# A sparse graph layer on one core: another order of sixteen units in the second stage, one early load of rows, an early drain of GpSimd and a last store by ScalarE

## The chip, the cores and the metric

The kernel runs on one core of a Trainium2 chip. Its time is the device time of one launch in microseconds; the median of three runs is 1491.0 us (1484.07 to 1491.29). The profile shown here is one more execution, which took 1490.79 us; its trace spans 1488.3 us from the first to the last instruction.

## What is computed

The reference, cut to what matters (x is 8 x 4096 x 256, adj is 4096 x 4096 with few entries that are not zero, W is 256 x 256, all float32):

```python
HW = einsum('bnf,fo->bno', x, W)
A_norm = relu((adj + adj.T) * 0.5)
D = sum(A_norm, axis=1)
DAD = D**-0.5 [:, None] * A_norm * D**-0.5 [None, :]
out = relu(einsum('nm,bmo->bno', eye(N) - DAD, HW))
result = layernorm(x + out, axis=-1)
```

Nodes with low numbers have many neighbours, nodes with high numbers few. The kernel uses that: for each block of output rows it gathers only the rows of HW that have an entry there.

## The kernel before, in words

**First stage** (to about 565 us). It reads adj, makes it symmetric, writes it to a buffer in HBM (`a_dram`), sums the degrees, forms g = r * (x W) for every block of 128 nodes and writes it to `g_dram` (8 KB for one node: 8 batches of 256). It also finishes the product of output block 0 (`lead`) and prepares the lists of the first units of `SEQ`.

**Second stage** (from about 565 us). The other 31 blocks of 128 output rows are taken in 16 *units*. Unit u has blocks 2u+1 and 2u+2, called b0 and b1 below; unit 15 has one block. They are taken in the order of the list `SEQ`; before the change that is 1 to 9, then 0, then 10 to 15. Low numbers are heavy, with 0 the heaviest.

- A unit needs `tiles` gathered tiles. A tile is 128 rows of g (`gather`, L959, 1 MB) and the matching pieces of adj (L951), both by indirect DMAs that GpSimd issues. Rows that a list doesn't fill aren't fetched. The tiles lie in a ring of `RING` = 12 buffers: `gather_ahead` asks for the next tile as soon as the oldest one has been used for the last time. Two "hub" blocks of g stay in SBUF.
- TensorE works a unit off in *steps*, in an order that `steps_of` fixes. A step is one full product of a tile (128x128, four banks), or a round in which up to eight small products of 64x32 run beside each other on parts of the array, with one to five tiles (`tiled`). Both are one pass over four PSUM banks. Blocks b0 and b1 have four banks each.
- When a block is complete, ScalarE evicts its four banks to y (`evict`, L767; there is one y buffer). VectorE adds the rows of x (L777), makes the statistics, the inverse root and the normalised rows (L786 to L810); SyncE stores them (`store`, L820). Rows of x come through `residual` (L761), issued by ScalarE into a pool of four buffers, the first block's after three steps of a unit and the second's after five (`after(6, ...)`, `after(10, ...)`; each step counts two).
- The lists of later units are made on the way. In the unit at place n of SEQ, VectorE runs `prepare` (patterns of the unit at n+4, and `spread` of that at n+2), and then, one step after b0 is complete, TensorE runs the counting products of `lists` (L293, L294, L376, L377, L430). They borrow two banks of b0. VectorE reads them (`index`, `place_rest`, `place`), and only then can the next unit's b0 begin. In the last places there is less of this: no patterns from place 12 on, and no lists at all from place 14 on.
- Every engine works in order, and `queue(...)` puts instructions behind the last one traced on an engine. ScalarE also carries a nop for each pass of a tiled step (`ticks`, L1201), which TensorE waits for two passes later.

**The end.** `finish_last` treats the last block in four parts: eviction by ScalarE, additions by GpSimd and VectorE, the inverse root by GpSimd (L1039), the normalisation by ScalarE (L1048), and one store for each part by SyncE (L1055). A flag is then read, which decides on a fallback that isn't taken with this input, and all engines drain and meet (L1323).

Of the kernel before, what the change touches and what calls it, by code (L numbers as in the profile page):

```python
# [20 lines left out]

KINDS = [15, 1, 4, 2, 8, 16, 64, 32, 128, 240, 51, 204, 60, 195, 0]

SEQ = [*range(1, 10), 0, *range(10, 16)]

HUBS = [2] * 16

# [40 lines left out]
def kernel(  # L68
# [25 lines left out]
    nc = tc.nc  # L94
    B, N, F = x.shape
    FO = w.shape[1]
    P = 128
# [6 lines left out]
    NU = NB // 2  # L104
# [4 lines left out]
    HOLD = 10  # L109
    RING = 12  # L110
    REACH = 5
    EPS = 1e-5
    NK = len(KINDS)
    L = 64
# [355 lines left out]
    with (  # L470
# [181 lines left out]

        due = [[n + 1, constants, (u,)] for n, u in enumerate(SEQ)]

# [43 lines left out]
        for i in range(NS):  # L698
            diag = stat1.tile([P, A, P], F32, tag="diag", name=f"diag_{i}")
            for j in range(i, NS):  # L700
                tij = load_adj(i, j)
                tji = load_adj(j, i) if j > i else tij
                parts = [(i, j, tij, tji)] + ([(j, i, tji, tij)] if j > i else [])
                parts = [(p, spool.tile([P, A, S], F32, tag="sym", name=f"sym_{p[0]}_{p[1]}")) for p in parts]
# [29 lines left out]
            if i in (1, 2, 3, 4):  # L734
                u = SEQ[i - 1]
# [6 lines left out]
            if i in (2, 4):  # L742
                u = SEQ[i // 2 - 1]
                at = 4 if i == 2 else 0
# [14 lines left out]
    def residual(i, engine):  # L759
        xr = blocks_pool.tile([P, B, F], F32, tag="adj", name=f"xr_{i}")  # L760
        engine.dma_start(xr, x[:, i * P : (i + 1) * P, :].rearrange("b p f -> p b f"))  # L761
        return xr
# [56 lines left out]
    def store(i, z):  # L819
        nc.sync.dma_start(out[:, i * P : (i + 1) * P, :].rearrange("b p f -> p b f"), z)  # L820
# [72 lines left out]
    with (  # L893
# [18 lines left out]
        steps = [(u, step) for u in SEQ for step in steps_of(u)]  # L912
# [14 lines left out]
        def queue(engine):  # L927

            traced = reversed(nc.cur_bb.bb.instructions)
            return tc.issue_after(next(i for i in traced if i.engine == engines[engine]))  # L930
# [38 lines left out]
        def gather_ahead():  # L969
            nonlocal asked, eaten  # L970
            while eaten < asked and not uses_left[order[eaten]]:
                eaten += 1
            while asked < len(order) and asked - eaten < RING:
                gather(asked)
                asked += 1
            if asked == len(order) and asked - eaten < RING and NB - 1 not in xr:
                xr[NB - 1] = ring[asked % RING].rearrange("p (b f) -> p b f", b=B)
                with queue("pool"):
                    nc.gpsimd.dma_start(
                        xr[NB - 1], x[:, (NB - 1) * P :, :].rearrange("b p f -> p b f")  # L980
                    )


        later = []

        def after(n, fn, *args):
            later.append((n, fn, args))
# [7 lines left out]

        u = SEQ[0]
        xr = {i: residual(i, nc.sync) for i in (0, *range(2 * u + 1, 2 * u + 1 + blocks(u)))}
# [10 lines left out]
        def finish_last(i):  # L1008

            z, banks = xr.pop(i), py.pop(i)  # L1010
            y = ypool.tile([P, B, FO], F32, tag="y", name=f"y_{i}", bufs=1)
            n = S // FO
            parts = [slice(c * n, (c + 1) * n) for c in range(G // S)]
            for c, bs in enumerate(parts):
                with queue("act"):
                    nc.scalar.activation(
                        y[:, bs].rearrange("p b o -> p (b o)"),
                        banks[c],
                        AF.Relu,
                        scale=minus_r[:, i : i + 1],  # L1020
                    )

            with queue("pool"):
                nc.gpsimd.tensor_add(z[:, parts[0]], z[:, parts[0]], y[:, parts[0]])
            with queue("dve"):
                nc.vector.tensor_add(z[:, parts[1]], z[:, parts[1]], y[:, parts[1]])
            stats = []
            for c in range(len(parts) + 1):
                if c < len(parts):
                    if c == 2:  # L1030
                        with queue("dve"):
                            nc.vector.tensor_add(z[:, parts[3]], z[:, parts[3]], y[:, parts[3]])
                    with queue("dve"):
                        mv, rstd = statistics(i, z[:, parts[c]], stat, f"_{c}")
                    if c == 0:
                        with queue("pool"):
                            nc.gpsimd.tensor_add(z[:, parts[2]], z[:, parts[2]], y[:, parts[2]])
                    with queue("pool"):
                        nc.gpsimd.tensor_tensor(rstd, rstd, neg_half[:, :n], ALU.pow)  # L1039
                    stats.append((mv, rstd))  # L1040
                if c == 0:
                    continue
                bs, (mv, rstd) = parts[c - 1], stats[c - 1]
                shift = stat.tile([P, n], F32, tag="shift", name=f"shift_{c - 1}")
                with queue("dve"):
                    nc.vector.scalar_tensor_tensor(shift, mv[:, :, 0], -1.0, rstd, ALU.mult, ALU.mult)
                for b in range(n):
                    nc.scalar.activation(  # L1048
                        y[:, bs.start + b, :],
                        z[:, bs.start + b, :],  # L1050
                        AF.Identity,
                        bias=shift[:, b : b + 1],
                        scale=rstd[:, b : b + 1],
                    )
                nc.sync.dma_start(out[bs, i * P : (i + 1) * P, :].rearrange("b p f -> p b f"), y[:, bs])  # L1055

        def finish(i):

# [22 lines left out]
        def exchange(rows):  # L1081

            if finished:
                with queue("sp"):
                    store(*finished.pop(0))
            for i in rows:
                with queue("act"):
                    xr[i] = residual(i, nc.scalar)


        ahead = {u: {k: SEQ[n + k] for k in (2, 3, 4) if n + k < NU} for n, u in enumerate(SEQ)}

        def prepare(u):
            if 2 in ahead[u]:
# [109 lines left out]
        for q, (u, step) in enumerate(steps):  # L1204
            new = q == 0 or steps[q - 1][0] != u
            if new:
                after(6, prepare, u)
                rows = [2 * u + 1 + b for b in range(2)] if q > 0 and blocks(u) == 2 else []
                if q == 0:
                    after(8, exchange, [])  # L1210
                elif rows:
                    after(6, exchange, rows[:1])
                    after(10, exchange, rows[1:])
                else:
                    after(2, exchange, [])
                    after(4, exchange, [])
                left, begun = {}, set()
                for v, st in steps[q:]:
                    if v == u:
                        for _, _, b, j in st:  # L1220
                            for e in range(QU) if j is None else [j]:
                                left[b, e] = left.get((b, e), 0) + 1
                for b in range(blocks(u)):
                    py[2 * u + 1 + b] = []
            touched = sorted({b for _, _, b, _ in step})
            for b in touched:
                if not py[2 * u + 1 + b]:
                    py[2 * u + 1 + b] = [
                        psum.tile([P, S], F32, tag=f"b{b}", name=f"py_{u}_{b}_{c}") for c in range(NC)
                    ]  # L1230
            if step[0][1] is None:
                (op,) = step
                b = op[2]
                hs = {(b, e) for e in range(QU)}
                assert not hs & begun or hs <= begun
                for h in hs:
                    left[h] -= 1
                for c in range(NC):
                    product(
                        u, op, c, slice(0, P), slice(0, P), not hs & begun, not any(left[h] for h in hs)  # L1240
                    )
                begun |= hs
            else:
                for op in step:
                    assert op[2:] in begun
                    left[op[2:]] -= 1
                last = [op for op in step if not left[op[2:]]]
                tiled(u, step, last)
            for op in step:
                t = op[0]  # L1250
                uses_left[u, t] -= 1
                if t < 0:
                    load_hub_rows(SEQ[SEQ.index(u) + 1 :], -1 - t, op[2])
            gather_ahead()
            run_later(2)
            for b in touched:
                if not any(left[b, e] for e in range(QU)):
                    if b == 0:
                        after(2, lists, u)
                    finish(2 * u + 1 + b)  # L1260
# [11 lines left out]
    with tc.If(short > 0):  # L1272
        with (
# [4 lines left out]
            for i in range(NB):  # L1278
# [16 lines left out]
                y = evict(i, py, ypool)  # L1295
# [32 lines left out]
```

## Time and profile before

| | |
|---|---|
| median of three runs | 1491.0 us |
| the profiled execution | 1490.79 us |
| its span | 1488.3 us |
| mean granted TensorE clock | 0.974 |
| moved by DMA | 541.85 MB, 364 GB/s over the span |

The second stage by units, in the order of SEQ. Tiles and steps follow from the tables `CAPS` and `FIRST` through `steps_of`. Start and length run from the first matmul of the unit to that of the next one. Idle is TensorE's idle time in it, V is VectorE's busy time, DMA the share of the 16 DMA engines.

| unit | tiles | steps | start us | length us | idle us | V us | DMA |
|---|---|---|---|---|---|---|---|
| 1 | 22 | 21 | 582.5 | 83.8 | 4.1 | 22.9 | 1.01 |
| 2 | 19 | 18 | 666.3 | 64.9 | 0 | 44.8 | 0.96 |
| 3 | 19 | 17 | 731.2 | 61.1 | 0 | 42.2 | 1.00 |
| 4 | 18 | 15 | 792.3 | 56.0 | 1.9 | 48.5 | 0.98 |
| 5 | 17 | 15 | 848.3 | 53.9 | 0 | 45.2 | 1.02 |
| 6 | 17 | 14 | 902.2 | 55.8 | 2.8 | 45.2 | 1.00 |
| 7 | 16 | 13 | 958.0 | 52.3 | 2.7 | 45.3 | 1.02 |
| 8 | 17 | 12 | 1010.3 | 51.3 | 3.4 | 45.9 | 1.00 |
| 9 | 16 | 12 | 1061.6 | 51.3 | 4.1 | 45.0 | 0.98 |
| 0 | 27 | 28 | 1112.9 | 107.2 | 3.3 | 44.9 | 0.92 |
| 10 | 14 | 12 | 1220.1 | 45.0 | 1.6 | 41.6 | 0.90 |
| 11 | 15 | 12 | 1265.1 | 49.5 | 5.8 | 45.6 | 1.00 |
| 12 | 15 | 11 | 1314.6 | 51.6 | 7.4 | 47.9 | 0.99 |
| 13 | 13 | 11 | 1366.2 | 39.5 | 0 | 26.7 | 1.02 |
| 14 | 13 | 11 | 1405.7 | 38.5 | 0 | 22.4 | 1.00 |
| 15 | 7 | 5 | 1444.2 | 24.2 | 2.8 | 14.6 | 0.63 |

How to read the profile: a page gives each engine's busy time, in tenths in 40 equal slices of the span too. "PEclk" is the clock that TensorE was granted. A row of the waits says which engine waited, at which line, for whom, how long in total, how often, and how long at most. A row of the timeline gives start, duration, engine, line and operation of instructions put together, and in brackets the idle time before them and what ended it. Ends of matmuls are modelled, so that a wait of TensorE can lie inside its busy time; the starts tell more.

### The profile page before, as it was taken

Reading aid. Unit: us, or ns where it says so; the run is one execution under the profiler, and the core shown is the slowest. Engines: PE = TensorE matmul, PEld = TensorE weight load, DVE = VectorE, ACT = ScalarE, POOL = GpSimd, SP = SyncE. Lnnn points to the kernel's source line nnn. Section 1 sums busy time; section 2 is a strip of 40 time slices with the busy share of each in tenths; the row PEclk is TensorE's granted clock in tenths of the full one; section 3 lists DMA queues with packets and bytes.
Section 4 is the critical chain, followed back from the end, with each engine's and each line's share of the span. In section 5 each row is a group of like instructions: output and inputs, shape, how many; then the busy total and the mean of one; then the engine's idle time right before and its main releaser. Section 6 shows DMA issues by size and latency. Waiting matters only on the chain.

```text
span 1488.3 us, 29574 instructions
## 1 busy us (share of the span) xinstructions
PE 1381.5 (93%) x10960; PEld 749.5 (50%) x10960; DVE 1042.9 (70%) x3174; ACT 360.8 (24%) x462; POOL 761.4 (51%) x1556
## 2 busy tenths in 40 slices
PE   7998988979998998999999999999989999988993
PEld 6777877756777763343433333333333334433341
DVE  4668569879687763219486897788889029999654
ACT  4555554444544460000101101100100010011111
POOL 2445010010322336765775777777767557777761
PEclk9999999999999999999999999999999999998996
DMA  9999999998999999999999999999999889999994
GB/s 348 364 377 380 403 365 358 387 388 314 357 361 354 368 388 379 390 400 337 370 379 358 375 401 374 382 394 378 348 387 386 312 292 383 370 352 398 393 369 144
DMA packets 216694, 541.85 MB, mean 364 GB/s; under 512 B 19070, under 2 KB 108862, under 8 KB 182110
## 3 DMA queue, kind: packets, MB, share of 16 engines
q0 software_dynamic: 55200, 282.68, 49.1%
q1 hardware_dynamic: 93472, 126.89, 24.7%
q10 hardware_dynamic: 67872, 130.32, 23.1%
q8 instruction: 89, 1.46, 0.4%
q14 instruction: 61, 0.50, 0.1%
HBM read 434.91 MB, written 136.34 MB: 384 GB/s over the span
## 4 chain that ended last, share of the span: by engine, by line
PE 53%; DMA 23%; DVE 16%; issue 5%; ACT 2%; POOL 1%; ACTq 0%; DVEq 0%; POOLq 0%
PE py L1166 33%; PE pg L606 9%; DMA g<-g_dram,gi 7%; DMA a_dram<-sym 6%; DVE sym L499 3%; PE lead L564 3%; PE tr L495 3%; PE xtr L595 3%; DMA xin<-in_x_dram 3%; DMA out_dram<-xr 2%; DMA xr<-in_x_dram 2%; DMA ga<-a_dram,ai 2%; DVE stats L786 2%; DVE xr L810 1%; DVE xr L777 1%
## 5 line engine op out<-in xcount | busy, mean ns | idle before, releaser
L1166 PE MATMUL py<-g,ga 64*32 64x512 f32 (+1 forms) x7072 | 612.4, 610 | 23.1 <-DMA g<-g_dram,gi 22.0
L1166 PEld LDWEIGHTS py<-g,ga 64*32 64x32 f32 (+1 forms) x7072 | 226.8, 114 | 392.1 <-issue 314.7
L959 POOL DMA_INDIRECT g<-g_dram,gi x265 | 297.7, 1124 | 113.6 <-issue 71.0
L951 POOL DMA_INDIRECT ga<-a_dram,ai x265 | 282.9, 1068 | 136.2 <-PE py L1166 64.1
L767 ACT ACTIVATE y<-py,minus_r 128x512 f32<-128x512 f32 x120 | 72.7, 688 | 789.1 <-PE py L1166 634.4
L606 PE MATMUL pg<-w_sb,xt 128*128 128x256 f32 x1024 | 229.7, 383 | 4.2 <-ACT xt L596 4.2
L1166 PE MATMUL py<-g_hub,gh 128*128 128x512 f32 x496 | 229.2, 604 | 3.8 <-DVE pos_k L239 3.8
L606 PEld LDWEIGHTS pg<-w_sb,xt 128*128 128x128 f32 x1024 | 194.8, 193 | 30.5 <-ACT xt L596 5.0
L499 DVE TENSOR_TENSOR sym<-tr,adj 128x512 f32<-128x512 f32 x256 | 162.8, 683 | 57.4 <-PE tr L495 40.6
L506 DVE TENSOR_REDUCE sums<-sym 128x64 f32<-128x2048 f32 x64 | 145.3, 2279 | 62.4 <-ACT sym L503 62.4
L1166 PEld LDWEIGHTS py<-g_hub,gh 128*128 128x128 f32 x496 | 91.2, 191 | 136.3 <-issue 123.5
L495 PE MATMUL tr<-ident,adj 128*128 128x128 f32 x1024 | 135.9, 280 | 21.4 <-DVE sym L499 14.8
L503 ACT ACTIVATE sym<-sym 128x2048 f32<-128x2048 f32 x64 | 122.6, 1915 | 113.6 <-DVE sym L499 101.2
L507 POOL TENSOR_SCALAR uses<-sums 128x64 uint8<-128x64 f32 x64 | 24.8, 388 | 239.5 <-DVE sums L506 203.5
L442 DVE TENSOR_SCALAR low<-lists 128x17 f32<-128x17 f32 (+8 forms) x14 | 2.5, 175 | 200.0 <-PE lists L430 200.0
L495 PEld LDWEIGHTS tr<-ident,adj 128*128 128x128 f32 x1024 | 115.2, 143 | 53.7 <-DVE sym L499 32.5
L777 DVE TENSOR_TENSOR xr<-xr,y 128x2048 f32<-128x2048 f32 x31 | 70.9, 2286 | 54.7 <-ACT y L767 42.0
L595 PE MATMUL xtr<-ident,xin 128*128 128x128 f32 x512 | 72.8, 291 | 21.3 <-DVE sym L499 12.3
L810 DVE TENSOR_SCALAR xr<-xr,mv,root 128x256 f32<-128x256 f32 x248 | 87.6, 425 | 1.1
L786 DVE BATCH_NORM_STATS2 stats<-xr 128x6 f32<-128x256 f32 x248 | 84.1, 412 | 1.1
L564 PE MATMUL lead<-gt,strip 128*128 128x512 f32 x176 | 83.2, 593 | 0.0
L596 ACT COPY xt<-xtr 128x512 f32<-128x512 f32 x128 | 68.0, 592 | 60.0 <-PE xtr L595 58.6
(157 smaller groups left out, 1057.7 us busy)
## 6 DMA issues: line engine op xcount, KB each, us to landing
adj<-in_adj_dram SPq DMA_DIRECT2D x64, 1024.0 KB, 10.2
a_dram<-sym ACTq DMA_DIRECT2D x64, 1024.0 KB, 8.9
out_dram<-xr SPq DMA_DIRECT2D x31, 1024.0 KB, 23.6
xr<-in_x_dram ACTq DMA_DIRECT2D x28, 1024.0 KB, 15.1
xin<-in_x_dram SPq DMA_DIRECT2D x44, 512.0 KB, 11.9
g_dram<-gt ACTq DMA_DIRECT2D x22, 1024.0 KB, 8.9
xin<-in_x_dram POOLq DMA_DIRECT2D x20, 512.0 KB
g_dram<-held ACTq DMA_DIRECT2D x10, 1024.0 KB, 14.1
```

The source lines that it names most:

```text
L495: ins = nc.tensor.transpose(pt[:, c * P : (c + 1) * P], tji[:, c, a * P : (a + 1) * P], ident)
L499: nc.vector.tensor_add(sym[:, a, :], pt, tij[:, a, :])
L503: nc.scalar.activation(sym, sym, AF.Relu, scale=0.5)
L506: nc.vector.tensor_reduce(sums, sym.rearrange("p a (c q) -> p a c q", q=E), AX.X, ALU.add)
L564: nc.tensor.matmul(lead[c], lhsT=strip, rhs=g[:, c * S : (c + 1) * S], start=not done, stop=len(done) == NB - 1, skip_group_check=True,)
L595: nc.tensor.transpose(pt[:, k, c, :], xin[b // H][:, b % H + k, c * P : (c + 1) * P], ident)
L606: ins = nc.tensor.matmul(pg[:, k * FO : (k + 1) * FO], lhsT=xt[:, b + k, c, :], rhs=w_sb[:, c, :], start=(c == 0), stop=(c == FC - 1),)
L786: nc.vector.bn_stats(stats[:, b, :], z[:, b, :])
L810: nc.vector.tensor_scalar(z[:, b, :], z[:, b, :], mv[:, b, 0:1], rstd[:, b : b + 1], ALU.subtract, ALU.mult,)
L951: nc.gpsimd.indirect_dma_start(out=at if both else at[:, : E if one else P], out_offset=None, in_=a_pairs if both else a_groups if one els ...
L959: nc.gpsimd.indirect_dma_start(out=gt, out_offset=None, in_=g_dram, in_offset=bass.IndirectOffsetOnAxis(ap=gi[:, t : t + 1], axis=0), boun ...
L1166: return nc.tensor.matmul(py[2 * u + 1 + b][c][cols, :], lhsT=at[ps, off + cols.start : off + cols.stop], rhs=gt[ps, c * S : (c + 1) * S], ...
```

## The change

Four edits.

1. `SEQ` takes the units in another order: 2, 4, 3, 5, 11, 7, 6, 1, 12, 0, 13, 10, 14, 9, 8, 15. The first stage follows, since it prepares the lists of the first four of them.
2. In a unit of at least `LONG` = 28 steps (only unit 0 has so many) both blocks of x of the unit behind it are loaded after 14 steps (`load_rows`, ScalarE's queue). `exchange` in that next unit still stores, and finds the rows there.
3. GpSimd gets a `drain` behind its last gathers and the load of the last block's rows.
4. The fourth and last store of `finish_last` is issued by ScalarE in place of SyncE.

```diff
-SEQ = [*range(1, 10), 0, *range(10, 16)]
+SEQ = [2, 4, 3, 5, 11, 7, 6, 1, 12, 0, 13, 10, 14, 9, 8, 15]
...
+    LONG = 28
...
                     nc.gpsimd.dma_start(
                         xr[NB - 1], x[:, (NB - 1) * P :, :].rearrange("b p f -> p b f")
                     )
+                with queue("pool"):
+                    nc.gpsimd.drain()
...
-                nc.sync.dma_start(out[bs, i * P : (i + 1) * P, :].rearrange("b p f -> p b f"), y[:, bs])
+                engine = nc.sync if c < len(parts) else nc.scalar
+                engine.dma_start(out[bs, i * P : (i + 1) * P, :].rearrange("b p f -> p b f"), y[:, bs])
...
+            load_rows(rows)
+
+        def load_rows(rows):
+
             for i in rows:
-                with queue("act"):
-                    xr[i] = residual(i, nc.scalar)
+                if i not in xr:
+                    with queue("act"):
+                        xr[i] = residual(i, nc.scalar)
...
-        ahead = {u: {k: SEQ[n + k] for k in (2, 3, 4) if n + k < NU} for n, u in enumerate(SEQ)}
+        ahead = {u: {k: SEQ[n + k] for k in (1, 2, 3, 4) if n + k < NU} for n, u in enumerate(SEQ)}
...
+                if sum(v == u for v, _ in steps) >= LONG:
+                    v = ahead[u][1]
+                    after(LONG, load_rows, [2 * v + 1 + b for b in range(2)])
```

## The prediction

> **What bounds the kernel now.** I read the page's slices first, then the second stage cut at the units' first matmuls, then the waits, then TensorE's timeline around each wait, and the last lines at the end. Slices (40 of 37.2 us):
>
> ```profile
> PE   7998988979998998999999999999989999988993
> DVE  4668569879687763219486897788889029999654
> PEclk9999999999999999999999999999999999998996
> DMA  9999999998999999999999999999999889999994
> ```
>
> The first stage barely depends on the edits, so I look at slices 15 to 39. DMA is at its top all the way but for slices 31 and 32 (the first is 0), where VectorE shows 0 and 2: that is unit 0 (1112.9 to 1220.1 us). Right behind it VectorE is at 9.
>
> The second stage by units (length, then busy us of each engine, clock, DMA share); the rows are units 8, 9, 0, 10, 11, 12, 13, 14:
>
> ```profile
> 1010.30:1061.60 51.30, 47.95 (x566) 17.75 (x564) 45.94 (x170) 4.84 (x8) 39.71 (x38) 0.97 1.00 379
> 1061.60:1112.90 51.30, 47.18 (x449) 18.38 (x445) 44.99 (x171) 4.84 (x8) 36.88 (x37) 0.97 0.98 361
> 1112.90:1220.10 107.20, 103.92 (x861) 39.42 (x860) 44.87 (x169) 4.84 (x8) 66.06 (x65) 0.98 0.92 345
> 1220.10:1265.10 45.00, 43.40 (x510) 19.00 (x508) 41.64 (x157) 4.84 (x8) 30.19 (x29) 1.00 0.90 344
> 1265.10:1314.60 49.50, 43.68 (x466) 19.66 (x462) 45.58 (x170) 4.84 (x8) 36.88 (x35) 0.99 1.00 373
> 1314.60:1366.20 51.60, 44.22 (x455) 17.59 (x451) 47.88 (x172) 4.84 (x8) 38.69 (x36) 0.87 0.99 375
> 1366.20:1405.70 39.50, 39.50 (x408) 15.79 (x401) 26.71 (x95) 4.93 (x9) 28.98 (x27) 1.00 1.02 392
> 1405.70:1444.20 38.50, 38.50 (x370) 14.93 (x369) 22.44 (x82) 6.35 (x11) 24.57 (x24) 1.00 1.00 369
> ```
>
> VectorE's work is about 45 us a unit, heavy or light, until the lists run out (units 13, 14). Who waits:
>
> ```profile
> DVE low L442 <- PE lists L430: 200.0, 14, 60.0
> PE py L1166 <- DMA g<-g_dram,gi: 22.0, 11, 3.5
> ```
>
> VectorE waits for TensorE 200 us in total, 60 of it in unit 0; elsewhere TensorE waits for it. TensorE's timeline:
>
> ```profile
> 993.42 8.65 PE L1166 MATMUL py<-g,ga 64*32 64x512 f32 x124 [2.69 <-DMA g<-g_dram,gi]
> ...
> 1047.77 5.34 PE L1166 MATMUL py<-g,ga 64*32 64x512 f32 x60 [2.66 <-DMA g<-g_dram,gi]
> ...
> 1264.26 0.95 PE L430 MATMUL lists<-val,hot 128*128 128x30 bf16 x32
> ...
> 1305.48 3.70 PE L1166 MATMUL py<-g_hub,gh 128*128 128x512 f32 x8
> 1313.29 0.36 PE L293 MATMUL lists<-kind,ones 128*128 128x448 bf16 x1 [4.11 <-DVE kind L283]
> ...
> 1313.73 0.99 PE L430 MATMUL lists<-val,hot 128*128 128x26 bf16 x32
> ```
>
> So three limits lie close together. **P**: unit 3 (17 steps, no wait) took 61.1 us; less about 1.25 for its lists that is 3.52 us a step, so P = 3.52 x steps + 1.25. **V**: behind unit 0 the lists of units 10, 11, 12 (L430 at 1215.8, 1264.3, 1313.7, 1359.2) follow at 48.4, 49.5 and 45.4 us, VectorE solid between them: no unit with full list work is shorter than about 48.5. **D**: from 582.5 to 1468.4 us the gathers' queue takes 76.6% of the DMA engines' time, 678 us for 265 tiles or 2.56 a tile; stores and row loads take 10.1 and 10.0%, 178 us for 31 blocks, 11.5 a unit.
>
> Last, the end's line L1323:
>
> ```profile
> L1323 POOLq DRAIN  x3: 46/103/8321, 1479.2 to 1488.1; - x3
> L1323 SPq DRAIN  x3: 7/7/7, 1485.3 to 1487.8; - x3
> ```
>
> GpSimd's drain runs from 1479.2 to 1487.5; SyncE, which waits for the last store, is through at 1485.4.
>
> **What the Trainium skill says.** "Perfetto Trace Analysis", Optimization Strategy: where the most-contended engine changes over time, interleaving the regimes may help. The trace agrees that there are such regimes (unit 0 against 10 to 12). "TensorE: Matmul & The Clock Gate", Part 1: after an idle window of about 3.4 us the array runs at half clock until it has been busy as long. It agrees: the step around the 2.69 us wait above took 8.4 us (989.7 to 998.1) at clock 0.80, against 3.5; a wait costs nearly twice its length. "DMA: Bandwidth & Descriptors", Queues, rings and completion order: the engines go round the queues. It agrees: from 1130 to 1140 us loads, gathers and stores had 38.4, 36.6 and 31.3%, where gathers had 96.9% from 1160 to 1180; a wait in unit 0 follows at 1148. No page prices GpSimd's drain.
>
> **The change, part by part.** Each sum is against the profiled 1490.8 us, which is practically the median.
>
> (a) *Places 0 to 9, up to the tenth lists.* Before: 582.5 to 1215.8, 633.3 us, with units 1 to 9 and 0, 165 steps. Ten units, nine lists' 1.25 and a last step behind the lists: 164 x 3.52 + 11.3 = 588.6, losses 44.7. They are: 8.8 at the start (first round, five tiles: 12.3 us for 3.5), 2.2 in unit 4 (VectorE, behind unit 3), 4.9, 4.8, 8.6, 7.1 and 7.0 in units 6, 7, 8, 9, 0 (gathers), and about 1.3 in small ones. After: units 11 and 12 for 8 and 9, one step less, 163 x 3.52 + 11.3 = 585.1. Losses: start 6.2 (unit 2's first round needs four tiles, and a tile's two issues take 2.57 us on GpSimd); 2.2 behind unit 3; 11 has P = 43.5 against V = 48.5, so 5.0; 12 has 40.0, so 8.5; 7 keeps its 4.8, since its tiles 125 and 126 could not be asked for before 979.2 and are used at 989.7; unit 6 2 (D = 17 x 2.56 + 11.5 = 55 against P = 50.5, with unit 11 and 7 ahead of it); unit 0 4, since its queue is fuller. Sum 32.7, so 617.8: **-15.5**. Bounds: losses of 24 to 45, so -24 to -3.
>
> (b) *Places 10 to 12.* Units 13, 10, 14 for 10, 11, 12: one step less, but VectorE's work belongs to the place and not to the unit. P is 40.0, 43.5, 40.0, all under V. 143.3 us remain: **0** (-3 to +3).
>
> (c) *Places 13 to 15.* Before: 1359.2 to 1468.4, 109.2 us. Units 9 and 8 in place of 13 and 14: two steps more, **+7.0**. D is 52.5 and 55.0 against P of 43.5: the queue falls 20 us behind, against 5.3 + 6.3 in units 13 and 14, which had no wait. The ring is 12 x 2.56 = 31 us deep and full after (b), but some of it isn't usable, since unit 9's tile 159 gets its buffer at 1082.9 and is needed at 1091.7. Units 9 and 8 lost 7.1 and 8.6 before; from a full queue I take 3 for each. **+13** in all (+7 to +22). Unit 15's own 6 us wait I leave.
>
> (d) *Rows of unit 13 in the middle of unit 0.* Two loads of 1 MB, 88.6 / 28 = 3.2 us of the DMA engines each, go where the share falls to 0.60 (1174 to 1188), and leave unit 13's start. Unit 13 waits for VectorE, so **0**. They stand in ScalarE's queue ahead of L1201's nops: if their buffers weren't stored by then, TensorE would stand. About 50 us into unit 0 the stores of the unit before are gone (gathers alone from 1160), which hides it; without that cover some 5 us.
>
> (e) *Drain.* It goes where GpSimd is idle from 1448.2 to 1469.3, 21 us for 8.3; behind it in its queue is only L1024. The second and third drain took 0.10 and 0.05 us, so I take the last one as short. SyncE then ends it: **-2.1** (0 if it costs 8.3 again).
>
> (f) *Last store by ScalarE.* SyncE issued it at 1480.55, 0.03 behind the last activation; it saves a semaphore and the queue behind the third store: **-0.1** (0 to -0.6).
>
> Sum: 1490.8 - 15.5 + 0 + 13 - 2.2 = **1486**.
>
> **Rivals.** *Forecast* (0.40): as above; own range 1479 to 1494. *The queue stays full* (0.30): (a) loses only 26 and reaches -22, and a full ring carries 9 and 8, (c) +8: 1490.8 - 22 + 8 - 2.2 = 1475. For it: DMA falls short only in units 2, 0, 10 and 15. Against: the waits of units 7 and 9 come from buffers, not from bandwidth. *Tail starves* (0.20), the slower side: 9 and 8 stand where no heavy unit follows; of the 20 us only some 10 are covered (unit 14 was 11.6 behind, and unit 15 waited), the rest costs nearly double through the clock. Then (c) is 7 + 16 = +23, and (a) about -11 for the same reason: 1490.8 - 11 + 23 - 2.2 = 1501. It decides once (c) exceeds (a)'s gain by 10. *The order does nothing* (0.10): VectorE's floor in places 4, 8 and 10 to 12 eats what unit 0 gave; only the end gains: 1489.
>
> **How the numbers follow.** A measurement here can tell about 0.5% (7.5 us) from no change: 1483.5 and 1498.5 are the borders. Faster: nearly all of the second case and a third of the first, 0.42. Slower: most of the third, 0.18. Same: 0.40. The range reaches from below the second case to the third: 1469 to 1502.
>
> **What would show it.** Lists at 48 to 50 us in places 4, 8, 10, 11; the tenth lists some 13 to 18 us earlier; TensorE waiting for gathers in units 9 and 8 near the end; GpSimd's last drain under 1 us. I am wrong if light units behind heavy ones run at 40 to 44 us between lists, or if 9 and 8 run at 43 us or above 55.

## The result, and the profile after

The changed kernel takes 1492.25 us (median of 17 runs, 1486.62 to 1498.57) against 1488.79 us for the kernel before (17 runs, 1484.07 to 1496.77): a ratio of 1.0038 [1.0025, 1.0051]. It is slower by some 0.4% (the two medians differ by 0.2%, 3.5 us), where 0.3% faster was forecast. The time lies inside the stated range, but on the other side of the kernel before. (Some experiments below ran where the kernel before itself took 1739 to 1743 us at a mean clock near 0.92 in place of 0.97, so each ratio holds only beside its own time of the kernel before, and most experiments stand twice, the second time beside 1484 to 1490 us.)

The profiled execution took 1492.11 us, with a span of 1490.0 us and a mean clock of 0.972. Cut as the prediction cuts it, in us of the two profiled executions (a *place* is a position in `SEQ`, counted from 0; places 0 to 9 are called the front below, places 13 to 15 the tail):

| stretch | before | after | difference | forecast |
|---|---|---|---|---|
| start of the second stage | 582.5 | 583.7 | +1.2 | 0 |
| (a) to the tenth lists | 633.4 | 624.0 | -9.4 | -15.5 |
| (b) to the thirteenth lists (places 10 to 12) | 143.3 | 142.9 | -0.4 | 0 |
| (c) to the last matmul | 109.2 | 124.2 | +15.0 | +13 |
| (e), (f) from there to the end | 20.0 | 15.2 | -4.8 | -2.2 |
| span | 1488.3 | 1490.0 | +1.7 | -4.7 |

The start of the second stage lies anywhere from 580 to 588 us in the profiles of these kernels, whose first stages hardly differ, so its 1.2 us mean nothing. The two spans differ by 1.7 us where the medians differ by 3.5: the sums below hold to a few us, and it is the two large entries, -9.4 and +15.0, that have to be explained.

The slices of the kernel after:

```profile
PE   7998998979999999999999999999979997998985
DVE  4667568789597752257958979965699058999417
PEclk9999999989999999999999999999989998998998
DMA  9999999999999999999999999999999978999995
```

The dip of DMA hasn't gone. From slices 31 and 32 it has moved to 32 and 33 (1192 to 1266 us), the end of unit 0 and the light unit 13. VectorE shows 0 in slice 31, inside unit 0, then 5, 8 and 9: in unit 13 the others wait for it, as the next two views show. The units 6, 12, 0, 13, 10, 14, 9, 8 and 15 of the kernel after (length, then busy us of PE, PEld, DVE, ACT and POOL, clock, DMA share, GB/s):

```profile
926.30:983.70 57.40, 54.06 (x486) 20.25 (x485) 45.07 (x169) 4.85 (x8) 42.08 (x41) 0.97 1.01 384
1059.70:1110.10 50.40, 41.27 (x454) 17.09 (x452) 46.02 (x173) 4.85 (x8) 35.91 (x34) 0.90 0.98 361
1110.10:1212.10 102.00, 101.47 (x869) 38.41 (x862) 44.07 (x169) 4.85 (x8) 61.01 (x60) 1.00 0.97 361
1212.10:1262.60 50.50, 42.05 (x405) 16.64 (x404) 46.17 (x171) 4.85 (x8) 33.59 (x30) 0.90 0.82 293
1262.60:1306.30 43.70, 43.34 (x510) 19.12 (x508) 40.38 (x156) 4.84 (x8) 30.47 (x27) 1.00 0.89 343
1306.30:1357.50 51.20, 42.59 (x408) 16.75 (x405) 47.40 (x172) 6.42 (x11) 37.02 (x36) 0.90 1.00 382
1357.50:1403.60 46.10, 43.83 (x441) 18.57 (x440) 26.81 (x96) 3.38 (x7) 28.57 (x27) 1.00 0.94 319
1403.60:1457.20 53.60, 48.92 (x529) 18.35 (x527) 22.83 (x83) 4.79 (x8) 39.90 (x39) 0.94 0.99 381
1457.20:1474.80 17.60, 17.60 (x128) 6.81 (x120) 16.33 (x69) 2.42 (x4) 0.00 (x0) 1.00 0.56 204
```

Units 13 and 14 took 39.5 and 38.5 us at the end of the old order, with 27 and 22 us of VectorE's work. In places 10 and 12 they take 50.5 and 51.2, with 46 and 47 of it. TensorE's timeline shows why (in order of time: a line of unit 6, one of unit 12, two of unit 13, two of unit 8):

```profile
963.85 11.62 PE L1175 MATMUL py<-g,ga 64*32 64x512 f32 x140 [2.76 <-DMA g<-g_dram,gi]
...
1104.01 0.56 PE L294 MATMUL lists<-kind,ones 128*128 128x448 bf16 x1 [9.13 <-DVE kind L284]
...
1243.58 3.70 PE L1175 MATMUL py<-g_hub,gh 128*128 128x512 f32 x8
1255.73 0.56 PE L294 MATMUL lists<-kind,ones 128*128 128x448 bf16 x1 [8.45 <-DVE kind L284]
...
1427.80 13.05 PE L1175 MATMUL py<-g,ga 64*32 64x512 f32 x170 [1.70 <-DMA g<-g_dram,gi]
...
1444.74 5.35 PE L1175 MATMUL py<-g,ga 64*32 64x512 f32 x60 [2.23 <-DMA g<-g_dram,gi]
```

In unit 13 TensorE stands 8.45 us until VectorE has the patterns for the lists (L284), and in unit 12 it stands 9.13 us. In units 6 and 8 it waits for gathers: 2.76, then 1.70 and 2.23 us. At the end, the drains of the kernel after (duration in ns, minimum, median and maximum, then first and last start):

```profile
L984 POOLq DRAIN  x1: 17057/17057/17057, 1453.9 to 1453.9; - x1
...
L1335 POOLq DRAIN  x3: 34/47/103, 1483.7 to 1489.7; - x3
L1335 SPq DRAIN  x3: 7/7/7, 1489.1 to 1489.5; - x3
```

The early drain (L984) takes 17.06 us, twice the 8.32 of the old one. It ends at 1471.0, and GpSimd's next work is at 1475.8, so it costs nothing. The first of the three at L1335, which took the 8.32 us before, takes 0.05 us.

**One balance for all orders.** Every order has the same 227 steps, so only losses differ. A unit's loss is what it took over 3.52 us a step and over the 1.25 us or so of the lists made in it. From the three profiles (the third is f3_tail_back, an experiment below):

| units | before | after | f3_tail_back |
|---|---|---|---|
| first unit (1; 2; 2) | 8.7 | 2.8 | 1.0 |
| the others of 1 to 5 | 2.0 | 3.4 | 2.7 |
| 6 and 7 | 10.5 | 12.9 | 11.5 |
| 8 and 9 | 15.6 | 14.3 | 16.9 |
| 0 | 7.4 | 2.2 | 2.6 |
| 10, 11, 12 | 19.1 | 17.4 | 19.0 |
| 13 and 14 | -0.4 | 21.8 | -0.4 |
| 15 | 6.6 | 0.0 | 3.6 |
| sum | 69.5 | 74.8 | 56.9 |

The change pays 22.2 us in units 13 and 14, and elsewhere it saves 16.9 on balance, chiefly in the first unit, in unit 0 and in unit 15.

### The profile page after: what moved, and what is told of

Read it like the earlier page. It is cut to its first block, busy times and chain, and to the rows that moved or that the text cites. A ratio compares the mean times of both kernels' runs of the same rounds, so it can differ in the third digit from the quotient of the medians.

```text
span 1490.0 us, 29565 instructions
## 1 busy us (share of the span) xinstructions
PE 1378.9 (93%) x10960; PEld 751.3 (50%) x10960; DVE 1041.4 (70%) x3174; ACT 360.7 (24%) x462; POOL 773.9 (52%) x1556
## 4 chain that ended last, share of the span: by engine, by line
PE 48%; DVE 23%; DMA 20%; issue 4%; ACT 2%; POOL 2%; ACTq 0%; DVEq 0%; POOLq 0%
PE py L1175 29%; DMA g<-g_dram,gi 9%; PE pg L607 8%; DMA a_dram<-sym 6%; PE lead L565 5%; DVE sym L500 3%; DMA xin<-in_x_dram 3%; PE tr L496 3%; PE xtr L596 3%; DVE stats L787 2%; DVE xr L778 2%; DVE xr L811 2%; DVE sums L507 2%; DVE hot L410 1%; DMA ga<-a_dram,ai 1%
## 5 line engine op out<-in xcount | busy, mean ns | idle before, releaser
L952 POOL DMA_INDIRECT ga<-a_dram,ai x265 | 295.4, 1115 | 139.5 <-PE py L1175 66.0
L960 POOL DMA_INDIRECT g<-g_dram,gi x265 | 295.2, 1114 | 111.7 <-issue 64.7
L811 DVE TENSOR_SCALAR xr<-xr,mv,root 128x256 f32<-128x256 f32 x248 | 84.2, 411 | 1.1
## 6 DMA issues: line engine op xcount, KB each, us to landing
a_dram<-sym ACTq DMA_DIRECT2D x64, 1024.0 KB, 10.9
```

Of the source, the lines that this page charges most:

```text
L811: nc.vector.tensor_scalar(z[:, b, :], z[:, b, :], mv[:, b, 0:1], rstd[:, b : b + 1], ALU.subtract, ALU.mult,)
L952: nc.gpsimd.indirect_dma_start(out=at if both else at[:, : E if one else P], out_offset=None, in_=a_pairs if both else a_groups if one els ...
L960: nc.gpsimd.indirect_dma_start(out=gt, out_offset=None, in_=g_dram, in_offset=bass.IndirectOffsetOnAxis(ap=gi[:, t : t + 1], axis=0), boun ...
```

## The experiments

The theory to be tested: the loss sits in the order of the places behind unit 0. VectorE's list work stays with the place, so light units put there are stretched, and units 9 and 8, which lose time to their gathers, do so at the end as well. The rivals: the transfers as a whole (stores and gathers) bind; or the edits at the end or the early rows cost what the order gave.

### The edits one by one

e1_end_only and f6_end_only, the same edit, the order and the rows as before:

```diff
-SEQ = [2, 4, 3, 5, 11, 7, 6, 1, 12, 0, 13, 10, 14, 9, 8, 15]
+SEQ = [*range(1, 10), 0, *range(10, 16)]
-    LONG = 28
+    LONG = 99
```

> The order of before, with GpSimd's early drain and the last store by ScalarE; no early load of rows. Theory (the change is a sum: front -9, middle 0, tail +15, end -3 to -5): from the last activation to the end 5.0 us in place of 7.8, so about -2.8 us, ratio 0.998. Rival (the end was shorter because VectorE had finished the last block but one earlier, not through the drain): that stretch stays near 7.8 us and the time within 1 us.

> The order of before, the early drain and the last store by ScalarE, no early load. Theory: the stretch behind the last matmul falls by the 2.9 us that separate kernels with and without these edits elsewhere (15.2 against 18.0), to about 17; ratio 0.998. Rival (the gain is VectorE's being done earlier in the new order): stretch 20 us, ratio 1.000.

Measured: e1 0.9988 [0.9967, 1.0009] (1739.88 us beside 1742.58 for the kernel before) and f6 0.9968 [0.9938, 0.9999] (1734.71 beside 1738.64). From the last matmul to the end both profiles have 15.1 us, against 18.0 in e2_order_only, f4_order_only and others that lack the two edits: -2.9 us. For f6 about 17 had been expected. The kernel before has 20.0 because VectorE is late there (see f3_tail_back), which it isn't in these two runs. The end alone wasn't timed beside 1490 us.

e2_order_only and f4_order_only, the new order alone in the kernel before:

```diff
-SEQ = [*range(1, 10), 0, *range(10, 16)]
+SEQ = [2, 4, 3, 5, 11, 7, 6, 1, 12, 0, 13, 10, 14, 9, 8, 15]
```

> The kernel before with nothing but the new order of units. Theory: front some 9 us shorter, tail (twelfth-place lists to the last matmul) 124 us in place of 109, end without the drain's gain: about +6 us, ratio 1.004. Rival (the order is good and the early load or the drain spoils it): ratio 1.000 or below.

> The kernel before with nothing but the new order. Theory: front some 9 us shorter, places 10 to 12 unchanged, tail 124 us, end 18 us: about +6 us, ratio 1.003 to 1.006. Rival (the early load or the drain spoils a good order): ratio 1.000 or below.

Measured: e2 1.0049 [1.0026, 1.0072] (1751.15 us beside 1742.58) and f4 1.0029 [1.0011, 1.0048] (1492.97 beside 1489.26). The order by itself is slower. f4_order_only's stretches are 621.4, 142.7, 124.1 and 18.0 us. The same order in the kernel after took 2.6 more in the first. All of it falls ahead of unit 0, where none of the other edits has acted yet, so (a) in a single profile is good to some 3 us only. The last stretch shows the old drain of 8.32 us again, at L1323 in this kernel:

```profile
L1323 POOLq DRAIN  x3: 46/103/8321, 1484.6 to 1493.5; - x3
```

e8_no_early_rows, the kernel after without the early rows:

```diff
-    LONG = 28
+    LONG = 99
```

> The kernel after without the early load of unit 13's rows in unit 0. Theory (unit 13 waits for VectorE, so its rows are not late either way): within 2 us of the kernel after; unit 13's interval 48 to 50 us. Rival (the early load costs or saves in unit 0 or 13): 3 us or more off, to be seen in these two intervals.

Measured: 1750.74 us beside 1739.17 for the kernel before; from one run of each nothing follows. The better evidence is f4_order_only, which lacks the early rows too: unit 0 loses 2.2 us in it as in the kernel after, and the stretches behind it are 142.7 and 124.1 against 142.9 and 124.2. Where the early rows act they cost and bring nothing that shows. One thing stays open. The end of the kernel after is 2.8 us shorter than that of f4_order_only, so its ratio should lie 0.2% lower. It lies 0.1% higher (1.0038 against 1.0029), and the two intervals taken together reach down to 0.14% lower at most. No run shows why.

### Front or tail

e3_tail_back and f3_tail_back keep the other edits and change the order alone: its front is near the new one, with 8 and 9 for 11 and 12, and places 10 to 15 are those of the kernel before.

```diff
-SEQ = [2, 4, 3, 5, 11, 7, 6, 1, 12, 0, 13, 10, 14, 9, 8, 15]
+SEQ = [2, 4, 3, 5, 8, 7, 6, 1, 9, 0, 10, 11, 12, 13, 14, 15]
```

> The kernel after with units 8 and 9 in places 4 and 8 (for 11 and 12) and 10 to 15 behind unit 0: order 2 4 3 5 8 7 6 1 9 0 10 11 12 13 14 15. Theory (what is lost is lost in the tail): tail back to about 109 us, front gain of 5 to 9 kept, end -3: about 1478 us, ratio 0.992 to 0.994. Rival (light units between heavy ones cost what unit 0 gives; the tail is only where it shows): front gain gone, ratio 0.998.

> The kernel after in the order 2 4 3 5 8 7 6 1 9 0 10 11 12 13 14 15. Theory (what is lost is lost in the tail): tail about 109 to 113 us, places 10 to 12 at 143 to 148, front 3 to 8 us shorter than before, end 15.2: ratio 0.992 to 0.996. Rival (light units among heavy ones take the front's gain): front as before or longer, ratio 0.998.

Measured: e3 1.0060 [1.0028, 1.0092] (1751.13 us beside 1742.58); f3 0.9932 [0.9909, 0.9955] (1479.16 beside 1489.26). Stretches of f3, in the order (a), (b), (c) and the end: 623.9, 143.7, 105.7 and 19.8 us. So the new front's -9.5 us stays, with 8 and 9 in it, and the tail is 18.5 shorter than in the kernel after, of which 4.6 are given back at the end. There VectorE is late. Its row additions for the last two blocks, and GpSimd's early drain, in f3_tail_back:

```profile
1452.29 2.29 DVE L778 TENSOR_TENSOR xr<-xr,y 128x2048 f32<-128x2048 f32 x1 [8.19 <-issue]
```

```profile
1465.16 0.69 DVE L1029 TENSOR_TENSOR g<-g,y 128x512 f32<-128x512 f32 x1
```

```profile
L984 POOLq DRAIN  x1: 20050/20050/20050, 1438.7 to 1438.7; - x1
```

The last matmul ends at 1458.5, and VectorE's addition for the last block comes only at 1465.16, 6.7 us later. The same addition in the kernel before and in the kernel after:

```profile
1472.50 0.68 DVE L1026 TENSOR_TENSOR g<-g,y 128x512 f32<-128x512 f32 x1
```

```profile
1476.33 1.28 DVE L1029 TENSOR_TENSOR g<-g,y 128x512 f32<-128x512 f32 x1 [1.81 <-ACT y L1019]
```

Before, it comes 4.1 us behind the last matmul (1468.4); after, 1.5 us behind (1474.8), and there VectorE has been waiting for ScalarE. The early drain of f3, 20.05 us this time, is over at 1458.8, before GpSimd's next work at 1459.4.

e4_front_back, f7_front_back and h2_front_back, the reverse: a front like the old one, the new tail.

```diff
-SEQ = [2, 4, 3, 5, 11, 7, 6, 1, 12, 0, 13, 10, 14, 9, 8, 15]
+SEQ = [1, 2, 3, 4, 5, 6, 7, 11, 12, 0, 13, 10, 14, 9, 8, 15]
```

> The kernel after with the front of before: order 1 2 3 4 5 6 7 11 12 0 13 10 14 9 8 15, so units 11 and 12 stand in places 7 and 8 and units 9 and 8 near the end. Theory: front 2 to 4 us shorter than before (one step less), tail 124 us, end -3 to -5: about +8 us, ratio 1.005. Rival (as above): the tail is neutral, ratio 0.997 to 0.999.

> The kernel after in the order 1 2 3 4 5 6 7 11 12 0 13 10 14 9 8 15: the front of before with 11 and 12 for 8 and 9, the tail of after. Theory (the tail costs 15 us, VectorE holds 11 and 12 at 49 us): front 627 to 632 us, places 10 to 12 143, tail 124, end 15: 4 to 8 us above the kernel before, ratio 1.003 to 1.006. Rival (the front's mixing costs, the tail is neutral): ratio below 1.000.

> The kernel after in the order 1 2 3 4 5 6 7 11 12 0 13 10 14 9 8 15: the front of before with 11 and 12 for 8 and 9, the tail of after. Theory (the tail costs 15 us, VectorE holds 11 and 12 at 49 us): front 627 to 632 us, places 10 to 12 143, tail 124, end 15: 4 to 8 us above the kernel before, ratio 1.003 to 1.006. Rival (the front's mixing costs, the tail is neutral): ratio below 1.000.

Measured: e4 0.9961 [0.9941, 0.9982] and f7 0.9959 [0.9940, 0.9977] (1735.59 us beside 1742.58, 1731.2 beside 1738.64); h2 1.0077 [1.0053, 1.0101] (1500.8 beside 1490.05). Stretches of h2: 628.1, 143.6, 124.2 and 15.3 us. The tail costs the same 15 us under either front, and the new front is worth some 4 us (628.1 against 624.0, with 3 us of scatter; 0.4% by the two ratios). e4 and f7 have the opposite sign to h2, as e3 has to f3, so these three say nothing of the case of 1490 us.

### VectorE or the transfers

e5_before_no_norm, e6_after_no_norm, f1_before_no_norm and f2_after_no_norm leave out work of VectorE, the inverse root and the normalisation of blocks 1 to 30, in the kernel before (e5, f1) and after (e6, f2):

```diff
-                with queue("dve"):
-                    rstd = inverse_root(i, var, stat)
...
-                in_turn(normalise, i, z, mv, rstd)
```

> The kernel before without the inverse root and the normalisation of blocks 1 to 30 (left out; their rows are stored as x + y), which takes about 5.9 us of VectorE a block, 11.8 a unit. Theory (VectorE sets the floor of 48.5 us between lists in places 10 to 12): the intervals there fall to 44 to 46 us, so these three places take about 132 in place of 143.3 us; places 6 to 9 keep their waits for gathers. About 1478 us. Rival (transfers set those intervals and VectorE is only as busy): they stay at 48 to 50 us and the time within 3 us.

> The same left out of the kernel after. Theory: places 4 and 8 (units 11 and 12) fall from 49.5 to about 44 and 42 us, places 10 to 12 (13, 10, 14) from 142.9 to 125 to 130; the tail keeps its 124. Then this kernel is some 6 to 12 us below the kernel before without the normalisation, about 1468: the new order would pay if VectorE had room. Rival (transfers set the intervals): nothing moves but the end, and it stays 2 to 5 us above.

> The kernel before without the inverse root and the normalisation of blocks 1 to 30 (left out; rows are stored as x + y), about 11.8 us of VectorE a unit. Theory (VectorE sets the floor of places 10 to 12): these three take about 132 us in place of 143.3; units 6 to 9 keep their waits for gathers. Some 10 us below the kernel before. Rival (transfers set those intervals): they stay at 48 to 50 us each, time within 3 us.

> The same left out of the kernel after. Theory: places 10 to 12 (13, 10, 14) fall from 142.9 to 125 to 132 us, units 11 and 12 in places 4 and 8 to 44 to 47; the tail keeps about 124. Then it is some 3 to 10 us below the kernel before without the normalisation: the order pays if VectorE has room. Rival (transfers set the intervals): nothing moves, and it stays 2 to 5 us above.

Measured: e5 1744.2 and e6 1747.37 us, single runs beside 1739.17. Beside 1489.26: f1 1487.14 us, 0.9986 [0.9964, 1.0008]; f2 1475.0 us, 0.9897 [0.9797, 0.9996], from two runs only, which both lie 9 us or more below the fastest of the 17 runs of the kernel after. The old order gains nothing from a lighter VectorE that can be told from zero, the new one 1.4% by the ratios (1.0038 to 0.9897; 0.4 to 2.4% by f2's interval). So with a lighter VectorE the new order pays, and as it stands it doesn't. TensorE's timeline of f2, the four products of lists that bound places 10 to 12, and the pattern product ahead of the second:

```profile
1201.11 0.95 PE L431 MATMUL lists<-val,hot 128*128 128x28 bf16 x32
...
1240.48 0.35 PE L294 MATMUL lists<-kind,ones 128*128 128x448 bf16 x1
1240.91 0.95 PE L431 MATMUL lists<-val,hot 128*128 128x26 bf16 x32
...
1287.57 0.96 PE L431 MATMUL lists<-val,hot 128*128 128x32 bf16 x32
...
1325.52 0.96 PE L431 MATMUL lists<-val,hot 128*128 128x34 bf16 x32
```

From lists to lists 39.8, 46.7 and 37.9 us, where the kernel after has 48.8, 48.9 and 45.2, and L294 has no wait ahead of it. Units 12, 13 and 14 lose 0.0, -0.2 and 1.5 us in place of 10.4, 10.6 and 11.2. Unit 11 keeps 6.2 of its 6.8, and 6, 0, 9 and 8 now lose more, 10.7, 8.4, 8.7 and 13.8. In f1 places 10 to 12 are 135.1 us, 8 shorter than before, and most of that is given back: the front is 2.7 and the tail 5.0 us longer. (The profile of f1 is that of its slowest run, 1493.03 us, so it may overstate what is given back.) Units 13 and 14 of f1:

```profile
1362.90:1407.60 44.70, 42.31 (x409) 17.71 (x402) 19.71 (x61) 4.98 (x9) 30.91 (x29) 0.96 0.99 385
1407.60:1453.80 46.20, 42.69 (x370) 16.79 (x369) 13.11 (x42) 6.51 (x11) 30.86 (x31) 0.96 1.01 380
```

At a DMA share of 0.99 and 1.01 they are 5 and 8 us longer than before, while unit 15 loses 5 us less: the old tail is close to the limit of its transfers.

g1_few_stores and h1_few_stores take most of the stores away: the kernel after stores one batch of eight for blocks 1 to 30.

```diff
-        nc.sync.dma_start(out[:, i * P : (i + 1) * P, :].rearrange("b p f -> p b f"), z)
+        nc.sync.dma_start(out[:1, i * P : (i + 1) * P, :].rearrange("b p f -> p b f"), z[:, :1])
```

> The kernel after, storing only the first of the eight batches of blocks 1 to 30 (seven eighths of these stores are left out), which takes some 5 us of the DMA engines a unit. Theory L (load: units 6 to 9 wait because the DMA engines are behind): unit 6's loss falls from 6.8 to 3 us or less, unit 8's from 11.4 to 6 or less, tail from 124 to 118; 10 to 14 us faster in all. Theory B (buffers: the tile's buffer comes free too late, whatever the load): losses of units 6, 7, 8, 9 within 1.5 us of before, tail 123 to 125, some 2 us faster.

> The kernel after, storing only the first of the eight batches of blocks 1 to 30 (seven eighths of these stores are left out), some 5 us less for the DMA engines a unit. Theory L (units 6 to 9 wait because the DMA engines are behind): unit 6's loss falls from 6.8 to 3 us or less, unit 8's from 11.4 to 6 or less, tail from 124 to 118; 10 to 14 us below the kernel after. Theory B (the tile's buffer comes free too late, whatever the load): losses of units 6, 7, 8, 9 within 1.5 us of before, tail 123 to 125, some 2 us below it.

Measured: g1 1.0037 [1.0014, 1.0060] (1746.02 us beside 1738.64); h1 0.9923 [0.9895, 0.9952] (1477.95 beside 1490.05). Units 11, 6, 13 and 8 of h1, then TensorE in its unit 8:

```profile
821.40:866.70 45.30, 43.79 (x460) 17.23 (x459) 42.02 (x157) 4.84 (x8) 34.08 (x33) 1.00 0.96 349
921.40:972.10 50.70, 50.70 (x485) 21.07 (x484) 43.73 (x168) 4.84 (x8) 39.06 (x39) 1.00 1.00 371
1199.20:1249.20 50.00, 41.43 (x405) 16.49 (x404) 45.67 (x171) 4.84 (x8) 32.65 (x30) 0.90 0.72 259
1389.30:1440.20 50.90, 46.98 (x529) 18.93 (x527) 22.98 (x83) 4.70 (x8) 39.20 (x38) 0.93 0.98 357
```

```profile
1415.65 13.51 PE L1175 MATMUL py<-g,ga 64*32 64x512 f32 x174 [3.67 <-DMA g<-g_dram,gi]
```

It tells the losses apart. Units 6 and 11 lose 0.3 and 1.8 us in place of 6.8 and 6.8, so what they waited for was transfers. That holds for the light unit 11 too, where VectorE had been reckoned with (in the kernel after TensorE's waits in it are 0.63, 0.45 and 2.64 us, all for gathers). Units 12, 13 and 14 keep 11.4, 10.1 and 10.9, with DMA at 0.72 in unit 13; they lost 1.5 us or less in f2, so here it is VectorE. Unit 8 keeps 8.7 of its 11.4, and unit 7 has 7.6 in place of 6.1, though most of the stores' bytes are gone. One thing that holds unit 8 is in GpSimd's timeline, here of the kernel after (L952 and L960 are the two requests of a tile):

```profile
1379.02 1.40 POOL L952 DMA_INDIRECT ga<-a_dram,ai  x1 [2.97 <-PE py L1175]
1380.73 2.02 POOL L960 DMA_INDIRECT g<-g_dram,gi  x1 [0.30 <-issue]
1383.05 0.95 POOL L952 DMA_INDIRECT ga<-a_dram,ai  x1 [0.31 <-issue]
1384.31 1.01 POOL L960 DMA_INDIRECT g<-g_dram,gi  x1 [0.30 <-issue]
1385.62 0.94 POOL L952 DMA_INDIRECT ga<-a_dram,ai  x1 [0.30 <-issue]
1386.87 1.00 POOL L960 DMA_INDIRECT g<-g_dram,gi  x1 [0.30 <-issue]
```

and its busy time in the stretch that follows:

```profile
1379.00:1434.70 55.70, 43.52 (x41) 0.97 0.98 358
```

GpSimd waits 2.97 us there for a buffer of the ring, which TensorE has not yet released; the request is one of unit 9's last, and all of unit 8's stand behind it. From then on GpSimd hardly stops: in the 55.7 us it is busy for 43.5, has 0.30 us between most of its requests, and waits once more for a buffer (1.15 us at 1424.68). A tile's requests follow those of the tile before at 2.56 us at best. So unit 8's 17 tiles want at least 43.5 us of GpSimd, where its 12 steps are 42.2 us of TensorE's work, and its last tile is asked for at 1433.7, 7.8 us before the step that needs it begins. In h1 the stretch looks the same (1366.0 after a wait of 2.51, then 0.30 between requests but for two of 1.35 and 0.56), and in the kernel before nearly so (979.5 after a wait of 2.97). So unit 8 brings its loss with it: 7.8, 10.1 and 11.4 us in places 7, 4 and 14 (before, f3, after).

That GpSimd's pace sets this loss isn't shown. The DMA engines are at 0.98 in the same stretch, in h1 too, and by the landings in the trace of the kernel after they fall behind GpSimd. (Some landing records are missing, so they are paired here with the requests from the last one back; the pairs fit the ends of TensorE's waits at 1427.80, 1441.46 and 1444.74 to 0.15 us.) Rows of g asked for from 1380 to 1395 landed about 6 us after the request was written, those asked for at 1418.64 after 8.0, and those of unit 8's last tile, at 1433.65, after 10.0. Had they landed after 6, they would have been there at about 1440.7, ahead of the 2.23 us wait that ended at 1444.74. Late requests and slow transfers both stand, and no kernel with cheaper requests or smaller gathers was tried.

### A better order

e7_fed_tail and f5_fed_tail put units 8 and 9 right behind unit 0 and end as before:

```diff
-SEQ = [2, 4, 3, 5, 11, 7, 6, 1, 12, 0, 13, 10, 14, 9, 8, 15]
+SEQ = [2, 4, 3, 5, 6, 7, 1, 10, 11, 0, 8, 9, 12, 13, 14, 15]
```

> The kernel after in the order 2 4 3 5 6 7 1 10 11 0 8 9 12 13 14 15: units 8 and 9, which need more from the DMA engines than from TensorE, stand right behind unit 0, where VectorE holds the places at 48.5 us and the ring is full; 13, 14, 15 end the stage as before. Theory: front 8 to 11 us shorter than before, places 10 to 12 as before (143 us), tail 109 us or less, end -3: some 12 us (0.8%) below the kernel before. Rival (the floors of light units in places 7 and 8 take the front's gain): within 3 us of the kernel before less the end's 3.

> The order 2 4 3 5 6 7 1 10 11 0 8 9 12 13 14 15 with the rest of the kernel after, timed: front 618 us, places 10 to 12 148, tail 113, end 15 as in its look: ratio 0.990 to 0.996. Rival (the look was a lucky run): 0.998 or above.

Measured: e7 1477.74 us in one run beside one of 1483.51; f5 1.0006 [0.9976, 1.0036] (1737.38 beside 1738.64), so the expected 0.990 to 0.996 was missed. Stretches of e7: 617.7, 148.1, 113.5 and 15.2 us. It has fewer losses in front, but unit 8 loses 7.2, 9 loses 5.1, and 14 in the tail loses 9.0. The best version that was timed with several runs beside 1490 us is f3_tail_back, 1479.16 us, which beats both kernels.

## Why the prediction was wrong

The step that failed is the size of the front's gain. Term (a) put the losses of places 0 to 9 after the change at 32.7 us, and they are 38.5; the front gained 9.4 us where 15.5 were forecast. That alone turns the sign: -9.4 + 13 - 2.2 is +1.4. The prediction had named rightly that VectorE holds the places behind unit 0 and that the tail gets longer; sizes were wrong, and for units 11 and 8 the cause too.

Of the 6.4 us between the forecast and the measured span difference, (a) makes +6.1, (c) +2.0, the start +1.2, (b) -0.4 and the end -2.6 (rounding aside). So the forecast lies as near as it does in part by luck: the end made up for more than (c) missed.

**(a) failed in its terms.** Too low: unit 6 at 2 measured 6.8, and h1 shows that it is the transfers' load (0.3 with few stores). The prediction had 55 us of transfers against 50.5 of TensorE's work there, and took only 2 of these 4.5, as if units 11 and 7 left a lead. Units 11, 12 and 7 at 5.0, 8.5 and 4.8 measured 6.8, 10.4 and 6.1. For 12 the cause was right (VectorE; 0.0 in f2) and only the size short. For 11 the cause was wrong: VectorE was named, and it is mostly transfers, with 1.8 left in h1 but 6.2 in f2. Units 4 and 1 add 1.7. Too high: the start at 6.2, measured 2.8, and unit 0 at 4, measured 2.2. As f4_order_only has 621.4 us for the same front, some 2.6 of the 6.1 may be scatter.

The prediction's price of a wait, nearly twice its length, fits the 2.69 us wait from which it was read, but not a long one. Unit 12's wait of 9.13 us comes with a loss of 10.4. The clock was at half for 10.2 us, from 1097.0 to 1107.2, but 7.0 of these lie inside the wait, where they cost nothing. And where the prediction says that the trace agrees with what it cites on the clock, that holds for the half clock and for how long it lasts (0.80 over 8.4 us is 3.4 us at half); the wait that brought it on shows as 2.69 us only, shorter than the idle window named there.

**(b) held.** 142.9 us for 143.3, with other units in it and one step less: VectorE's work belongs to the place. f2 shows it from the other side (124.4 once VectorE is lighter).

**(c) was near in sum by luck, through two errors.** Unit 9's 3 us measured 2.9. Unit 8's 3, taken "from a full queue", measured 11.4. Its tiles can't be asked for before a request of unit 9 gets its buffer, and from there GpSimd asks almost without a pause and the last tiles still come too late; the prediction had no term for that. (How it divides between GpSimd's pace and the transfers is open, as said above.) Unit 15's own wait, 6.6 us, was left in and vanished: its seven tiles are asked for while unit 8 stands. 7.0 + 2.9 + 11.4 - 6.6 = 14.7, and 0.4 are units 13 and 14, which had been 0.4 under their steps.

**(d)**: 0 agrees with f4_order_only's stretches. **(e), (f)**: -2.9 us in place of -2.2, by the kernels with and without them; how it divides between the two wasn't tried. The early drain was taken at 8.3 us and takes 17.1, within the 21 us of cover that the prediction named. A further 2 us of the end came from VectorE, which is late for the last block in the profile of before and not in that of after (see f3_tail_back).

**The rivals.** "The queue stays full" had unit 8 carried by a full ring and (a) at -22; with 11.4 and -9.4 it is refuted. "The tail starves" has the right place and sign, with 15 us where it asked for 23. "The order does nothing" named VectorE's floor as what eats unit 0's gain, and that is near the cause: in places 10 to 12 units 13, 10 and 14 pay 22.0 us (10.6, 0.2 and 11.2) where 10, 11 and 12 paid 19.1, and 11 and 12 go on paying in places 4 and 8 (11 for the transfers).

## What to carry to other kernels

When the order of the work is changed, sort each loss by what it belongs to: to a place (here VectorE's list work in places 10 to 12), to a unit (unit 8's gathers, in every place where it was tried), or to a neighbourhood (unit 0's, unit 15's). In this case only the last kind was won by reordering; light work belongs where the work of the place has run out, as f3_tail_back shows. And where one engine writes the requests of all gathers, reckon its time a tile (here 2.56 us at best) beside the bytes and the buffers.

## What was not expected of the hardware

A drain of GpSimd can last long, and the profile doesn't show what it waits for. It took 8.32 us at the old end, 31 us after GpSimd's last request, and 0.05 us at the same point of the program when another drain had gone before. The early ones took 17.06 and 20.05 us. Those began while the last requests were still being written, so how much of them is a wait for these isn't separated.

TensorE's clock made long waits a little longer again: in units 12, 13 and 14 of the kernel after, with waits of up to 9.13 us, the mean clock was 0.90, where unit 10 between 13 and 14 had 1.00.
